# Splitting an inverse transform and a projection into groups of 16 passes among other matrix products

## The chip, the core and the metric

The kernel runs on one core of one Trainium2 chip. The metric is the device time of one execution in microseconds (us); three runs of the kernel before gave 5190.26 us in the median (5189.91 to 5219.42). The engines carry the profile's names: PE is TensorE (matrix products; PEld its weight loads), DVE is VectorE, ACT is ScalarE, POOL is GpSimd, SP the engine that here only issues loads and stores. Each engine runs its instructions in the order in which the program writes them.

## What is computed

Two layers on an image batch of 4 x 64 x 256 x 256 in fp32. The first, which the change touches, is a normalised convolution block with products in the frequency domain of 8 x 8 patches:

```python
def layer0(x):                                   # x: (4, 64, 256, 256)
    y = group_norm(x)
    hidden = einsum('bchw,oc->bohw', y, w1)      # 1x1, 64 -> 384 channels
    hidden = depthwise_3x3(hidden, w_dw)
    q, k, v = split(hidden, 3, axis=1)           # 128 channels each
    out = irfft2(rfft2(patches(q)) * rfft2(patches(k)))
    out = layer_norm_over_channels(unpatch(out)) * ln_w + ln_b
    return x + einsum('bchw,oc->bohw', v * out, w_out)   # projection and residual
```

The second layer is a GRU that runs column by column over the result; nothing of it changes.

## The kernel before

**Blocks.** Layer 0 runs over 32 blocks of 32 image rows (the GRU follows it). A block holds 128 patches, 64 in each half of the partitions; xq is its normalised input with a border of one pixel, 100 numbers for each 8 x 8 patch.

**Stages of a block, in the order of TensorE's program.** The loop `for n in range(NBLK + 1)` does, for block n:

1. *First chunk of 1x1 units.* Sixteen calls of `pointwise` (`unit_of`): 16 passes each (a product in fp32 is two passes in the trace, so 8 products), then one copy of 1024 numbers per partition from the ring into h. ACT makes most copies, DVE units 3 and 9. DVE meanwhile runs steps of block n-1's layer norm, one for each `go()`.
2. *`circular(n, 0, ..)`.* Four rounds of `products`: two `transform`s of 64 passes with matrices t from memory (depthwise filter and Fourier transform in one), a copy by ACT, two multiplications by DVE. `inverse` turns a pair of these products into z: 48 passes of 512 columns into four banks, then one ACT copy of 2048 numbers. The first of a block's four inverses runs in this stage.
3. *Second chunk of units*, with half 0 of block n-1's projection after unit 11 (`project`, then `add_residual` on DVE, then `leave`), and the second inverse after unit 15.
4. *`circular(n, 1, ..)`* with the third inverse in it. The fourth waits in the list `pending`.
5. *Third chunk of units*, for v. `flush()` after unit 3 runs the fourth inverse. DVE copies units 4, 6 and 15. The steps of `go()` at units 6 and 7 are statistics of z, 16 instructions each, and they need the z of the fourth inverse.
6. *Half 1 of block n-1's projection*, 64 passes of 512 columns from v of block n-1, then `go(1)`, `add_residual(1, ..)`, `go(3)`. The first of these steps closes the statistics (moments) and makes the first of eight passes over z (subtract the mean, multiply by the reciprocal deviation, in quarters).
7. *v's products.* Eight calls of `values` of 64 passes each with matrices t; `keep_values` copies them by ACT, k = 0 and 1, 3 and 4, 6 and 7 in one copy of 2048 numbers, k = 2 and 5 alone. Among them ACT and DVE normalise the next block's input (`normalize`), and `leave` makes statistics of the finished half and stores it.

**The ring.** All results of stages 1 to 7 go through one PSUM tile `psring` of eight banks, given out in turn by `psum(banks)`: two banks for a unit, a transform or a v product alone, four for an inverse, a projection or two v products. A request for four starts at bank 0 or 4. A bank is written again when its last reader is done, so with pairs in turn TensorE can be four units ahead of their copies.

**h, z, v** are single buffers. A v product k reads 16 of h's 128 channels for all units, and part b of a projection reads a quarter of v (32 features), which the products 2b and 2b + 1 of the new block overwrite.

**Order.** `InOrder` keeps every engine's instructions in program order, and as all of them are recorded by its one helper, every row of the profile has its line, L157. The rows are told apart by their tiles: `psring<-w_sb,xq` is a unit, `psring<-h,t` with 32 columns of weights a transform and with 64 a v product, `psring<-wk,g_sb` the inverse, `psring<-v,wo_sb` the projection. `wk<-psring,wk` of 512 columns is `add_residual`, and of 1024 the products.

Of the kernel before, what the change touches and what calls it, by code (L numbers as in the profile page):

```python
# [18 lines left out]
P = 128  # L19
# [6 lines left out]
NBLK = B * W // 32  # L26
# [136 lines left out]
def tile_conv_then_gru(  # L163
# [47 lines left out]
    with tc.tile_pool(name="xa", bufs=5) as xa, tc.tile_pool(name="sta", bufs=1) as sta, tc.tile_pool(  # L211
# [18 lines left out]
        for i in range(32):  # L230
# [3 lines left out]
            for k in range(4):  # L234
                at = slice(32 * k, 32 * k + 9)
# [40 lines left out]
    with layer0 as s:  # L276
# [1 line left out]
        tp = s.enter_context(tc.tile_pool(name="tp", bufs=4))  # L278
        ps2 = s.enter_context(tc.tile_pool(name="ps2", bufs=1, space=PSUM))
        ring = ps2.tile([P, 8, 512], F32, tag="ring", name="psring")  # L280
        place = [0]

        def psum(banks=2):

            at = place[0] + (-place[0]) % banks
            place[0] = (at + banks) % 8
            return ring[:, at % 8 : at % 8 + banks]

# [41 lines left out]
        def matrix(n, kind, k):  # L330

            fetch(n * 24 + order.index((kind, k)) + 4)
            return matrices.pop((n, (kind, k)))

        def unit_of(n, chunk, unit, vector):

# [21 lines left out]
        def pointwise(n, chunk, unit, vector):  # L358

            unit_of(n, chunk, unit, vector)()  # L360
# [53 lines left out]

        def flush():
            while pending:
                pending.pop(0)()

        def inverse(n, pair):

            pz = psum(4)
            for i in range(2):
                slot = PAIRS[pair % 2][i]
                both = wk[:, slot : slot + 2].rearrange("p t (r s g n) -> p r g t s n", r=2, g=2, n=NJ)
                for part in range(2 - i):
                    for g in range(2):
                        for c in range(4):
                            at = slice(32 * c, 32 * c + 32)
                            nc.tensor.matmul(
                                pz[g * 64 : g * 64 + 64, c].rearrange("p (t s n) -> p t s n", t=2, n=NJ),  # L430
                                lhsT=g_sb[at, part, i, :],
                                rhs=both[at, part, g],
                                start=i == part == 0,
                                stop=i == 1,
                                tile_position=(32 * c, g * 64),
                            )
            nc.scalar.copy(
                z[:, :, 32 * pair : 32 * pair + 32], pz.rearrange("p c (f n) -> p n (c f)", n=NJ)
            )

        def values(n, k, pv):

# [12 lines left out]
        def keep_values(k, count, pv):  # L455
            nc.scalar.copy(
                v[:, :, 16 * k : 16 * (k + count)], pv.rearrange("p x (f n) -> p n (x f)", n=NJ)
            )
# [78 lines left out]
            return xr  # L537

        def project(n, u):
            po = psum(4)  # L540
            y = v.rearrange("p n (b k) -> p b n k", k=32)
            for b in range(4):
                for r in range(4):
                    for s in range(2):
                        n0 = 32 * u + 16 * s
                        nc.tensor.matmul(
                            po[s * 64 : s * 64 + 64, r].rearrange("p (n k) -> p n k", k=32),
                            lhsT=wo_sb[32 * r : 32 * r + 32, b, :],
                            rhs=y[32 * r : 32 * r + 32, b, n0 : n0 + 16],
                            start=b == 0,  # L550
                            stop=b == 3,
                            tile_position=(32 * r, s * 64),
                        )
            return po

        def add_residual(u, po, xr):
            for g in range(2):
                grid = xr[g].rearrange("p (h r) (n c) -> p h n r c", h=2, c=8)
                for half in range(2):
                    nc.vector.tensor_tensor(  # L560
                        grid[:, half],
                        po[:, 2 * g + half].rearrange("p (n r c) -> p n r c", r=4, c=8),
                        grid[:, half],
                        ALU.add,
                    )
# [34 lines left out]
        def go(steps=1):  # L600
            for _ in range(steps):
                if norm:
                    next(norm, None)

        for n in range(NBLK + 1):
            last = n == NBLK
            more = not last and n // 8 + 1 < B
            if last:
                for _ in norm:
                    pass  # L610
                for i in range(4):
                    gated(n - 1, i)
                for u in range(2):
                    xr = residual(n - 1, u)
                    add_residual(u, project(n - 1, u), xr)
                    leave(n - 1, u, xr)
                break
            if more:
                look(n, 0)
            for unit in range(16):  # L620
                if unit < 14:
                    pointwise(n, 0, unit, unit in (3, 9) if norm else unit % 2)
                elif unit == 14:
                    last_two = [unit_of(n, 0, unit, False)]
                else:
                    last_two.append(unit_of(n, 0, unit, False))
                    for span in ((0, 16), (16, P)):
                        for copy in last_two:
                            copy(*span)
                if unit in (0, 3, 6, 9, 12):  # L630
                    go()

            def beside_first(sp):
                if n and sp < 3:
                    gated(n - 1, sp)
                go()
                if n and sp == 3:
                    gated(n - 1, sp)
                if more and sp == 1:
                    count(n, 0)  # L640

            go()
            circular(n, 0, beside_first)
            crossed(1)
            go(8)
            xr = [None, None]
            if n:
                xr[0] = residual(n - 1, 0)
            for unit in range(16):
                pointwise(n, 1, unit, unit in (7, 12))  # L650
                if n and unit == 11:
                    add_residual(0, project(n - 1, 0), xr[0])
                if n and unit == 13:
                    leave(n - 1, 0, xr[0])
                if more and unit == 9:
                    count(n, 4)
            flush()
            norm = layer_norm(n)

            def beside(sp):  # L660
                go()
                if more and sp == 2:
                    count(n, 8)

            circular(n, 1, beside)
            image = None
            if n:
                xr[1] = residual(n - 1, 1)
            for unit in range(16):
                pointwise(n, 2, unit, unit in (4, 6, 15))  # L670
                if more and unit == 2:
                    count(n, 12)
                    if n % 8 == 7:
                        t = wk[:, 3]
                        nc.gpsimd.dma_start(t[:, 0 : 2 * P].rearrange("p (a q) -> p a q", a=2), sums)
                        image = norm_of_pieces(nc, st0, t, lambda: psum()[:, :, 0], eps, sc0[:, n // 8 + 1])
                if image and unit in (4, 8, 12):
                    next(image)
                if unit == 3:
                    flush()  # L680
                if unit in (6, 7):
                    go()
                if unit % 4 == 3 and n + 1 < NBLK:
                    load(n + 1, unit // 4)
            po = project(n - 1, 1) if n else None
            go(1)
            if n:
                add_residual(1, po, xr[1])
            go(3)
            for k in range(8):  # L690
                if k in (0, 3, 6):
                    pv = psum(4)
                    values(n, k, pv[:, 0:2])
                elif k in (1, 4, 7):
                    values(n, k, pv[:, 2:4])
                    keep_values(k - 1, 2, pv)
                else:
                    pv = psum()
                    values(n, k, pv)
                    keep_values(k, 1, pv)  # L700
                if k in (1, 2, 4) and n + 1 < NBLK:
                    normalize(n + 1, k // 2)
                if k == 5 and n:
                    leave(n - 1, 1, xr[1])
                if k == 5 and n + 1 < NBLK:
                    normalize(n + 1, 3)
                if k in (6, 7):
                    go()
            fetch(n * 24 + 28)
# [251 lines left out]
```

## Time and profile before

| | us |
|---|---|
| median of 3 runs | 5190.26 |
| the profiled execution | 5200.96 |
| its span, first to last instruction | 5199.2 |
| TensorE clock granted, mean | 0.99 of full |

The profile is one execution. A busy share is a share of that span; a TensorE row shows when passes start and how long each takes to pass through, and passes on different tiles of the array overlap, so its end is modelled. In the timeline, consecutive instructions of one kind are one row: start, length from the first start to the last end, how many, and in brackets the idle time before the row and what ended it. The sums of TensorE by kind, over all blocks:

| passes | count | mean of one, ns |
|---|---|---|
| 1x1 units | 24576 | 273 |
| transforms | 32768 | 274 |
| v's products | 16384 | 223 |
| inverse | 6144 | 600 |
| projection | 4096 | 607 |

And the copies and additions beside them:

| | count | mean, ns |
|---|---|---|
| ACT h, whole unit (1024) | 1243 | 1029 |
| ACT h, 896 and 128 of a unit | 64 and 64 | 916 and 276 |
| DVE h, whole unit | 229 | 1214 |
| ACT z of an inverse (2048) | 128 | 1866 |
| ACT v, two products (2048) | 96 | 1867 |
| ACT v, one product (1024) | 64 | 1002 |
| DVE add_residual, each of four | 256 | 682 |
| DVE pass over a quarter of z | 256 | 2279 |

### The profile page before, as it was taken

To read this page: it belongs to the slowest core of one execution; us is meant where nothing else is said; L and a number is where in the kernel's file an instruction comes from. 1 tells how busy PE (TensorE), PEld (TensorE's weight loads), DVE (VectorE), ACT (ScalarE), POOL (GpSimd) and SP (SyncE) were. 2 spreads that over 40 slices of the span, in tenths; PEclk is the share of its full clock that TensorE was granted. 3 is DMA by queue.
4 is the path that set the end of the run, shared out by engine and by line. 5 is a ranking of instruction groups with operands and counts; after the bars stand their busy time and mean duration, and the time that the engine had idled before them with its cause. 6 is when DMAs were issued, how large, how long until landed. Compare 5 with 4: busy or idle time off the path is not lost.

```text
span 5199.2 us, 275863 instructions
## 1 busy us (share of the span) xinstructions
PE 4911.1 (94%) x127092; PEld 4202.2 (81%) x127092; DVE 4038.0 (78%) x7000; ACT 3348.7 (64%) x4253; POOL 1724.5 (33%) x1723
## 2 busy tenths in 40 slices
PE   4999999999999999999999999999789999999999
PEld 3887888788888888888887888888578888888888
DVE  4678888877888887788887777878667777777777
ACT  3666667666666766666666666667466666666665
POOL 0233333333333333333333323223333333333333
PEclk9999999999999999999999999999899999999999
DMA  7566665666666666666656656655443333333332
GB/s 266 148 171 178 185 180 166 168 175 169 171 188 173 171 170 175 172 178 180 186 160 162 151 155 164 168 159 151 111 123 99 100 98 99 100 100 100 97 100 71
DMA packets 421174, 784.55 MB, mean 151 GB/s; under 512 B 32604, under 2 KB 295552, under 8 KB 417632
## 3 DMA queue, kind: packets, MB, share of 16 engines
q1 hardware_dynamic: 366464, 533.76, 38.1%
q0 software_dynamic: 53264, 232.55, 15.3%
q8 instruction: 997, 16.33, 1.4%
q14 instruction: 161, 1.32, 0.1%
q10 hardware_dynamic: 288, 0.58, 0.0%
HBM read 622.72 MB, written 144.05 MB: 147 GB/s over the span
## 4 chain that ended last, share of the span: by engine, by line
PE 78%; DVE 7%; issue 5%; ACT 5%; DMA 4%; POOL 1%; ACTq 0%; POOLq 0%; SPq 0%; DVEq 0%
PE psring L157 57%; PE pshz L157 7%; PE pshr L157 6%; PE psni L157 5%; PE pshn L157 3%; DMA t<-t_all 2%; ACT z L157 2%; DVE n L157 2%; ACT v L157 1%; DVE wk L157 1%; ACT xq L157 1%; DVE st L157 1%; DVE g L157 1%; DVE z L157 1%; DMA wk<-in_sums 1%
## 5 line engine op out<-in xcount | busy, mean ns | idle before, releaser
L157 PEld LDWEIGHTS psring<-h,t 100*32 100x32 f32 x49152 | 1383.5, 119 | 249.1 <-issue 195.7
L157 PE MATMUL psring<-h,t 100*32 100x128 f32 x49152 | 1464.3, 257 | 96.7 <-issue 59.0
L157 PEld LDWEIGHTS psring<-w_sb,xq 64*100 64x100 f32 x24576 | 1372.6, 164 | 123.1 <-issue 89.7
L157 PE MATMUL psring<-w_sb,xq 64*100 64x128 f32 x24576 | 1430.4, 273 | 34.2 <-issue 21.6
L157 ACT COPY h<-psring 100x1024 f32<-100x1024 f32 (+2 forms) x1371 | 1234.1, 988 | 336.8 <-PE psring L157 335.9
L157 DVE TENSOR_TENSOR wk<-psring,wk 128x1024 f32<-128x1024 f32 (+1 forms) x768 | 759.5, 1037 | 461.5 <-PE psring L157 320.2
L157 POOL TENSOR_TENSOR v<-v,z 128x2048 f32<-128x2048 f32 x128 | 582.7, 4557 | 658.6 <-DVE wk L157 603.0
L157 DVE TENSOR_TENSOR z<-z,moments 128x2048 f32<-128x2048 f32 x256 | 578.0, 2279 | 2.3
L157 POOL TENSOR_TENSOR wk<-wk 128x1024 f32<-128x1024 f32 x128 | 303.4, 2371 | 618.7 <-DVE wk L157 596.6
L157 POOL TENSOR_TENSOR raw<-raw,st 128x512 f32<-128x512 f32 x256 | 303.1, 1184 | 530.6 <-DVE st L157 471.5
L157 ACT COPY z<-psring 128x2048 f32<-128x2048 f32 x128 | 238.9, 1866 | 348.8 <-PE psring L157 248.2
L157 PE MATMUL pshr<-st,wi 64*64 64x144 f32 (+7 forms) x12240 | 429.7, 269 | 6.7 <-DVE st L157 6.7
L157 DVE COPY h<-psring 100x1024 f32<-100x1024 f32 x229 | 277.5, 1214 | 198.7 <-PE psring L157 192.7
L157 PE MATMUL psni<-st,wi 64*64 64x144 f32 (+7 forms) x12240 | 428.6, 269 | 1.3 <-issue 1.3
L157 PE MATMUL pshz<-st,wi 64*64 64x144 f32 (+7 forms) x12240 | 428.8, 269 | 0.1
L157 ACT ACTIVATE z<-pshz,b_rz 128x288 f32<-128x288 f32 (+7 forms) x510 | 242.0, 475 | 281.3 <-PE pshz L157 275.8
L157 ACT COPY wk<-psring 128x1024 f32<-128x1024 f32 x256 | 259.5, 1014 | 249.5 <-PE psring L157 214.4
L157 DVE BATCH_NORM_STATS2 lnst<-z 128x6 f32<-128x128 f32 x2048 | 416.8, 282 | 0.0
L157 ACT COPY v<-psring 128x2048 f32<-128x2048 f32 (+1 forms) x160 | 243.3, 1521 | 251.0 <-PE psring L157 251.0
L157 PEld LDWEIGHTS pshr<-st,wi 64*64 64x64 f32 x12240 | 370.0, 133 | 41.1 <-DVE st L157 9.8
L157 PEld LDWEIGHTS psni<-st,wi 64*64 64x64 f32 x12240 | 369.7, 133 | 31.3 <-issue 0.7
L157 PE MATMUL psring<-wk,g_sb 32*64 32x512 f32 x6144 | 382.1, 600 | 9.2 <-issue 5.9
(96 smaller groups left out, 6170.2 us busy)
## 6 DMA issues: line engine op xcount, KB each, us to landing
t<-t_all SPq DMA_DIRECT2D x768, 400.0 KB
xq<-in_xh POOLq DMA_DIRECT2D x128, 800.0 KB, 6.1
wk<-in_x SPq DMA_DIRECT2D x256, 256.0 KB
x<-wk POOLq DMA_DIRECT2D x256, 256.0 KB, 5.4
seen<-in_x POOLq DMA_DIRECT2D x96, 512.0 KB, 7.6
raw<-x SPq DMA_DIRECT2D x128, 256.0 KB
raw<-x SPq DMA_DIRECT2D x256, 128.0 KB
out<-raw SPq DMA_DIRECT2D x128, 256.0 KB
```

The source lines that it names most:

```text
L157: return self.tc.keep_in_program_order(got(*args, **kwargs))
```

## The change

Three things are rearranged; no arithmetic is added or left out.

- `inverse` and `project` become generators that stop after every 8 products (16 passes). The fourth inverse of a block is issued in three groups, after units 3, 4 and 5 of the third chunk, and its copy to z follows the third. Half 1 of the projection is issued in four: one after unit 15, and one each after v's products k = 0, 2 and 4. `add_residual` follows the fourth; `go(4)` stands in one piece before v's products, and `leave` moves from k = 5 to k = 6. Elsewhere the generators run through at once.
- While an inverse or a projection is open, its four banks are held and `psum()` gives the other four in turn, two pairs; `release()` sets the turn on.
- v's products take two banks each and are copied one by one; the next block's normalisations stand at k = 0, 2, 4. The copies of units 14 (ACT) and 15 (DVE) of the third chunk are each made in two parts, channels 0 to 15 of both first, as the first chunk's are already.

```diff
-        place = [0]
+        place, held, turn = [0], [None], [0]
 
-        def psum(banks=2):
+        def psum(banks=2, hold=False):
 
+            if held[0] is not None:
+                at = (held[0] + 4) % 8 + 2 * turn[0]
+                turn[0] ^= 1
+                return ring[:, at : at + banks]
             at = place[0] + (-place[0]) % banks
+            if hold:
+                held[0], turn[0] = at % 8, place[0] % 4 // 2
             place[0] = (at + banks) % 8
             return ring[:, at % 8 : at % 8 + banks]
...
+        def release():
+            place[0] = (held[0] + 4) % 8 + 2 * turn[0]
+            held[0] = None
...
         def flush():
             while pending:
-                pending.pop(0)()
+                for _ in pending.pop(0)():
+                    pass
 
         def inverse(n, pair):
 
-            pz = psum(4)
+            pz = psum(4, True)
...
+                    yield
             nc.scalar.copy(
                 z[:, :, 32 * pair : 32 * pair + 32], pz.rearrange("p c (f n) -> p n (c f)", n=NJ)
             )
+            release()
...
         def project(n, u):
-            po = psum(4)
+            po = psum(4, True)
...
-            return po
+                yield po
...
                 if n and unit == 11:
-                    add_residual(0, project(n - 1, 0), xr[0])
+                    for po in project(n - 1, 0):
+                        pass
+                    add_residual(0, po, xr[0])
+                    release()
...
             for unit in range(16):
-                pointwise(n, 2, unit, unit in (4, 6, 15))
+                if unit < 14:
+                    pointwise(n, 2, unit, unit in (4, 6))
+                else:
+                    last_two = (last_two if unit == 15 else []) + [unit_of(n, 2, unit, unit == 15)]
+                if unit == 15:
+                    for span in ((0, 16), (16, P)):
+                        for copy in last_two:
+                            copy(*span)
...
                 if unit == 3:
-                    flush()
+                    spread = pending.pop(0)()
+                if unit in (3, 4, 5):
+                    next(spread)
+                if unit == 5:
+                    for _ in spread:
+                        pass
...
-            po = project(n - 1, 1) if n else None
-            go(1)
+            parts = project(n - 1, 1) if n else None
             if n:
-                add_residual(1, po, xr[1])
-            go(3)
+                next(parts)
+            go(4)
             for k in range(8):
-                if k in (0, 3, 6):
-                    pv = psum(4)
-                    values(n, k, pv[:, 0:2])
-                elif k in (1, 4, 7):
-                    values(n, k, pv[:, 2:4])
-                    keep_values(k - 1, 2, pv)
-                else:
-                    pv = psum()
-                    values(n, k, pv)
-                    keep_values(k, 1, pv)
-                if k in (1, 2, 4) and n + 1 < NBLK:
+                pv = psum()
+                values(n, k, pv)
+                keep_values(k, 1, pv)
+                if k in (0, 2, 4) and n:
+                    po = next(parts)
+                if k in (0, 2, 4) and n + 1 < NBLK:
                     normalize(n + 1, k // 2)
-                if k == 5 and n:
+                if k == 4 and n:
+                    add_residual(1, po, xr[1])
+                    release()
+                if k == 6 and n:
                     leave(n - 1, 1, xr[1])
                 if k == 5 and n + 1 < NBLK:
                     normalize(n + 1, 3)
```

More of the change, by code (lines that the diff above doesn't have):

```diff
@@ L614, in tile_conv_then_gru @@
                     xr = residual(n - 1, u)
-                    add_residual(u, project(n - 1, u), xr)
+                    for po in project(n - 1, u):
+                        pass
+                    add_residual(u, po, xr)
+                    release()
                     leave(n - 1, u, xr)
@@ L679, in tile_conv_then_gru @@
                 if unit == 3:
-                    flush()
+                    spread = pending.pop(0)()
[3 more added lines that the diff above has]
+                    for _ in spread:
+                        pass
                 if unit in (6, 7):
@@ L684, in tile_conv_then_gru @@
                     load(n + 1, unit // 4)
-            po = project(n - 1, 1) if n else None
-            go(1)
+            parts = project(n - 1, 1) if n else None
             if n:
-                add_residual(1, po, xr[1])
-            go(3)
+                next(parts)
+            go(4)
             for k in range(8):
-                if k in (0, 3, 6):
-                    pv = psum(4)
-                    values(n, k, pv[:, 0:2])
-                elif k in (1, 4, 7):
-                    values(n, k, pv[:, 2:4])
-                    keep_values(k - 1, 2, pv)
-                else:
-                    pv = psum()
-                    values(n, k, pv)
-                    keep_values(k, 1, pv)
-                if k in (1, 2, 4) and n + 1 < NBLK:
+                pv = psum()
[4 more added lines that the diff above has]
+                if k in (0, 2, 4) and n + 1 < NBLK:
                     normalize(n + 1, k // 2)
-                if k == 5 and n:
+                if k == 4 and n:
+                    add_residual(1, po, xr[1])
+                    release()
+                if k == 6 and n:
                     leave(n - 1, 1, xr[1])
```

## The prediction

> **What bounds the kernel now.** I read the page's engine line and chain of waits first, then the groups kept apart by shape, then the timeline of one block (1992 to 2046 us), last the start times of single passes in it.
>
> ```profile
> PE 4911.1 (94%) x127092; PEld 4202.2 (81%) x127092; DVE 4038.0 (78%) x7000; ACT 3348.7 (64%) x4253; POOL 1724.5 (33%) x1723
> PE 78%; DVE 7%; issue 5%; ACT 5%; DMA 4%; POOL 1%; ACTq 0%; POOLq 0%; SPq 0%; DVEq 0%
> ```
>
> TensorE sets the end over most of the span; VectorE is the next share of the chain. Averages do not show where, so here are the two groups of weight loads that the change touches, with their idle time:
>
> ```profile
> L157 PEld LDWEIGHTS psring<-w_sb,xq 64*100 64x100 f32 x24576 | 1372.6, 164 | 123.1 <-issue 89.7 <-ACT z L157 10.9 <-DVE h L157 7.4
> L157 PEld LDWEIGHTS psring<-h,t 100*64 100x64 f32 x16384 | 491.9, 138 | 71.8 <-issue 54.7 <-ACT v L157 12.7 <-DMA t<-t_all 2.0
> ```
>
> Waits for a copy out of the ring are small: 10.9 (the inverse's z), 7.4 (units copied by VectorE), 12.7 us (v's copies), 31.0 in all. "issue" has no releaser and stays. Now the stretch itself, TensorE, ScalarE and VectorE:
>
> ```profile
> 1994.16 2.83 PE L157 MATMUL psring<-wk,g_sb 32*64 32x512 f32 x48
> 1996.92 1.99 PE L157 MATMUL psring<-w_sb,xq 64*100 64x128 f32 x32
> 1997.15 1.86 ACT L157 COPY z<-psring 128x2048 f32<-128x2048 f32 x1 [1.74 <-PE psring L157]
> 1999.07 2.10 PE L157 MATMUL psring<-w_sb,xq 64*100 64x128 f32 x32 [0.15 <-ACT z L157]
> ...
> 2002.37 6.37 DVE L157 BATCH_NORM_STATS2 lnst<-z 128x6 f32<-128x128 f32 x32
> ...
> 2008.95 3.69 PE L157 MATMUL psring<-v,wo_sb 32*64 32x512 f32 x64
> 2009.13 1.22 DVE L157 COPY h<-psring 100x1024 f32<-100x1024 f32 x1 [0.39 <-ACT h L157]
> ...
> 2011.95 2.23 DVE L157 TENSOR_TENSOR z<-z,moments 128x2048 f32<-128x2048 f32 x1
> 2012.57 15.79 PE L157 MATMUL psring<-h,t 100*64 100x64 f32 x512
> 2014.10 2.47 DVE L157 TENSOR_TENSOR wk<-psring,wk 128x512 f32<-128x512 f32 x4
> 2016.49 6.81 DVE L157 TENSOR_TENSOR z<-z,moments 128x2048 f32<-128x2048 f32 x3
> ...
> 2023.21 2.47 DVE L157 BATCH_NORM_STATS2 bn<-wk 128x6 f32<-128x512 f32 x4
> ...
> 2025.71 0.37 DVE L157 BATCH_NORM_AGGREGATE st<-bn 128x2 f32<-128x48 f32 x1
> 2026.00 1.04 DVE L157 TENSOR_SCALAR xq<-xq,sc 128x1600 f32<-128x1600 f32 x1
> ...
> 2026.96 6.81 DVE L157 TENSOR_TENSOR z<-z,moments 128x2048 f32<-128x2048 f32 x3
> 2028.29 15.06 PE L157 MATMUL psring<-w_sb,xq 64*100 64x128 f32 x256
> ...
> 2033.69 1.22 DVE L157 COPY h<-psring 100x1024 f32<-100x1024 f32 x1
> ```
>
> To see: from unit 15's copy (2009.13) to the copy of unit 3 of the next block (2033.69) VectorE has no gap. Unit 7 of that block needs unit 3's ring pair. Call t the start of the last 1x1 pass (2008.75): unit 3's copy ends at t+26.16. Over the blocks measured so (29) that end has the median t+26.16 and unit 7 starts at t+26.93: VectorE is under 0.8 us from binding.
>
> **The change part by part** (us per block; 32 blocks, 31 with a projection in them).
>
> *More changes between tile shapes.* Passes are the same in number. The inverse becomes I16 U16 I16 U16 I16: two more pairs of changes 1x1-inverse. The projection becomes four groups with v's products between: three more pairs. Start to start the inverse takes 2.76 (1994.16 to 1996.92), the projection 3.62 (2008.95 to 2012.57): 16 passes more cost 0.86, so the inverse has 2.76 - 3 x 0.86 = 0.18 that is no passes. By single starts a 1x1 stretch has as much: after a 1x1 pass the next shape comes 0.200 later and not 0.103 (+0.10), its second round of eight +0.05, after the last inverse pass the 1x1 comes 0.518 later and not 0.38 (+0.14), its second pair +0.08: 0.37 a pair of changes. Projection to v: +0.14 and +0.05; v to another shape is only seen going to 1x1, 0.152 for 0.052 (+0.10), and +0.05 in the first round: 0.34. Cost 2 x 0.37 x 32 = 23.5 and 3 x 0.34 x 31 = 31.6, sum 55. The Trainium skill (TensorEngine Tiling (Array Packing), Key Properties) says that a change of tiling mode drains TensorE; that speaks against the change but gives no price. A sum that left it out would be -31 (the waits alone); with the rows it is +24. I take the rows. Bounds of v-to-projection, unseen in this order: 0 to 0.15 more, that is 0 to +14 us.
>
> *Waits removed.* z's 10.9 and VectorE's 7.4: units 4 and 5 now lie inside the inverse, but its copy starts two units later and the held half leaves units two pairs: unit 8 asks for z's banks. By starts, z's copy (1.86) ends some 0.2 after unit 8 could start, so I count half: -9. v's 12.7 goes wholly: eight single copies (1.00 each) for three of 1.87 and two of 1.00, 8.0 for 7.6 on ScalarE, +0.4 that its idle before (5.12 at 2016.57) covers.
>
> *Units 14 and 15 in halves.* ScalarE pays 276 + 916 ns for the 1029 of a whole copy, +0.16; VectorE has no such row, between 0 and +0.3, I take 0.15. Both lie beside part one of the projection and v's first product; without that cover they would delay the first v product, which starts at t+1.25 where the first halves should be done at t+0.7 and the unit-14 banks free at t+1.1.
>
> *Moved queues.* Normalisations at k = 0, 2, 4 instead of 1, 2, 4: xq's load was issued 17 us earlier (1995.51) and lands in 6.1; nothing. leave's four x stores on POOL pass one memset of 0.12, its statistics pass xq's scaling on VectorE; SP's order of loads is unchanged. Nothing.
>
> *The add waits longer, and VectorE queues behind it.* Before, add_residual reads the projection at t+5.34, long after it is done. Now its fourth part follows v's k = 4. From single starts: first v product t+1.25; a v product 1.90, a part with its changes 1.20; k = 1, 3 and 5 start at 4.34, 9.34, 14.29; the fourth part's last pass ends at t+14.4. VectorE by then has done unit 15's copy (1.35), the moments (1.7) and four scalings (2.24 each), so it stands from t+12.3: idle 2.1. Behind the add (2.39 to its successor) are xq's scaling 0.96, the statistics 2.79, three scalings 6.73, then unit 3's copy 1.22: it ends at 14.4 + 14.1 = t+28.5 against 26.16. TensorE could start unit 7 at t+26.3 and waits to 28.55. Unit 9's copy ends 5.49 later (two VectorE operations and itself), t+34.0, and unit 13 waits for it, starting at 34.05 against a median of 32.17 and a mean of 32.60 before. Stalls without releaser in k = 0 to 4 add 0.16 in the mean. So +1.6 in the mean (+1.9 by the median) x 31 = 50 to 58. This already contains the projection's changes and v's waits, which lie under it. Later VectorE has 0.5 in hand at the next transform, still 0.2.
> A rule weighs here: TensorE: Matmul & The Clock Gate (Architectural detail) says that VectorE's queue is strictly first in, first out. If scalings could pass the waiting add, only the TensorE sum (+24) would stand; with the rule the add holds them. The trace's VectorE order is the program's at every step, so I take the rule.
>
> *Sum.* VectorE's chain +54, the inverse's changes +23.5, its waits and VectorE's -9, rest of the ScalarE pacing in those 12 units about -6 (they take 12.16 in the mean, 11.02 at best, the like 12 of the second chunk 10.66): +62. The profiled execution took 5200.96 (span 5199.2), 0.2% over the median of 5190.26; the sum is a difference, so it stands on the median: 5252.
>
> **Rivals.**
> - *TensorE alone counts* (VectorE finds time, for instance because the fourth part ends earlier). +55 for changes, -31 waits: 5214. For: chain 78% TensorE. Against: no VectorE gap in the stretch.
> - *Not slower: the inserted groups fill waits.* Place: units 6 to 15 of the third chunk and v's products, where TensorE waits on copies. The 12 units exceed 10.66 by 1.5 in the mean, v's products their least by 0.87 (16.59 to 15.72): 2.4 x 32 = 76. If all of that is the ring's, -76 + 55 = -21: 5169. It decides when over 1.75 a block vanish and the add isn't late. Against: most of that excess is "issue" or loads.
> - *Worse:* the held half also stalls v or units (a unit waits when its pair's copy is late, about 0.5 a block): 5275.
> - That the change does not do what it says, I exclude: order on each engine is the program's.
>
> **How the numbers follow.** VectorE's chain 0.62 (5235 to 5270), TensorE alone 0.17, filled waits 0.11, worse 0.10. About 1%, 52 us, is what a measurement can tell from no change, so 5242 and 5138 are the limits. VectorE's case lies to about three quarters above 5242, with the worse one 0.56 slower; faster by over 1% needs more than every wait: 0.04; the rest 0.40 within. The range leaves out the filled waits and the far end of the worse case: 5195 to 5285; the likeliest case alone is 5235 to 5270.
>
> **What would show it.** Right: add_residual's VectorE row now has idle time before it, released by TensorE, some 2 us a block (60 in all); "DVE h" in the 1x1 weight-load row grows from 7.4 to over 60; "ACT v" in v's row goes to nearly 0; between groups of 16 passes the start-to-start time is 1.05. Wrong: VectorE still without a gap there, or unit 7 starting below t+27.5; then the sum falls to TensorE's. If a group of 16 costs under 0.9 start to start, the drain term is too large.

## The result, and the profile after

The changed kernel takes 5289.55 us in the median of six runs (5278.2 to 5306.63), the kernel before 5199.66 (six runs, 5189.91 to 5219.42): 1.0172 times as long, 95% interval 1.0149 to 1.0196. It is 90 us slower where 62 were forecast, and lies 4.5 us beyond the range. The 5252 of the forecast stood on the 5190.26 of three runs of the kernel before; of the 37.5 us between 5252 and 5289.55, 9.4 are that starting point and 28 the forecast itself. The profiled execution (span 5304.9) is the slowest of the six, so its difference to the profiled execution before is larger, 105.7.

The page's engine line and its chain of waits, after:

```profile
PE 4958.9 (93%) x127092; PEld 4196.9 (79%) x127092; DVE 4045.1 (76%) x7032; ACT 3384.3 (64%) x4381; POOL 1722.1 (32%) x1723
PE 71%; DVE 15%; issue 5%; DMA 5%; ACT 2%; POOL 1%; ACTq 0%; SPq 0%; POOLq 0%; DVEq 0%
PE psring L157 51%; PE pshz L157 7%; PE pshr L157 6%; PE psni L157 5%; DVE z L157 3%; PE pshn L157 3%; DMA t<-t_all 3%; DVE wk L157 3%; DVE bn L157 2%; DMA seen<-in_x 2%; DVE n L157 2%; ACT z L157 2%; DVE st L157 1%; DVE g L157 1%; DVE h L157 1%
```

The passes are as many as before, and VectorE is hardly busier. But its share of the chain went from 7% to 15%, and two names are new among its lines: `DVE bn` (statistics of rows) and `DMA seen` (the load of the next image's rows). The groups by shape say who waited (busy us, mean ns, then idle us before the group and what ended it). First three rows after, then the row of add_residual before:

```profile
L157 PEld LDWEIGHTS psring<-w_sb,xq 64*100 64x100 f32 x24576 | 1384.8, 166 | 240.0 <-DVE h L157 102.9 <-issue 94.7 <-ACT h L157 26.0
L157 PEld LDWEIGHTS psring<-h,t 100*64 100x64 f32 x16384 | 492.1, 138 | 116.4 <-issue 84.6 <-ACT h L157 25.2 <-ACT v L157 5.4
L157 DVE TENSOR_TENSOR wk<-psring,wk 128x512 f32<-128x512 f32 x256 | 159.1, 683 | 243.2 <-PE psring L157 126.5 <-issue 108.9 <-DMA wk<-in_x 7.8
```

```profile
L157 DVE TENSOR_TENSOR wk<-psring,wk 128x512 f32<-128x512 f32 x256 | 158.8, 682 | 176.1 <-issue 114.5 <-PE psring L157 53.8 <-DMA wk<-in_x 7.8
```

In the units' row the wait for VectorE's copies grew from 7.4 to 102.9; in v's row the wait for ScalarE's copies of v fell from 12.7 to 5.4. The 25.2 for `ACT h` there is new, but it is idle time of weight loads beside the projection's first group: v's first product starts at t+1.24 in every block, as forecast (1.25). Before add_residual VectorE now waits 126.5 for TensorE (53.8 before). The timeline of one block shows how they hang together (rows of TensorE and VectorE; t, the start of the block's last 1x1 pass as in the forecast, is 3344.13):

```profile
3344.33 1.11 PE L157 MATMUL psring<-v,wo_sb 32*64 32x512 f32 x16
3345.37 2.09 PE L157 MATMUL psring<-h,t 100*64 100x64 f32 x64
...
3347.41 9.08 DVE L157 TENSOR_TENSOR z<-z,moments 128x2048 f32<-128x2048 f32 x4
...
3357.24 1.11 PE L157 MATMUL psring<-v,wo_sb 32*64 32x512 f32 x16
...
3358.36 2.48 DVE L157 TENSOR_TENSOR wk<-psring,wk 128x512 f32<-128x512 f32 x4 [1.87 <-PE psring L157]
...
3364.03 6.36 PE L157 MATMUL psring<-w_sb,xq 64*100 64x128 f32 x112
...
3364.57 6.75 DVE L157 TENSOR_TENSOR z<-z,moments 128x2048 f32<-128x2048 f32 x3
...
3371.24 1.22 DVE L157 COPY h<-psring 100x1024 f32<-100x1024 f32 x1
...
3372.51 5.49 PE L157 MATMUL psring<-w_sb,xq 64*100 64x128 f32 x96 [2.12 <-DVE h L157]
```

VectorE has done its four passes at 3356.5 and stands until the projection's fourth group (3357.24) is through, 1.87 us. Everything behind the add is late by that, unit 3's copy too, and TensorE stands 2.12 us before unit 7 (x112 is seven units).

From the starts of single passes, means over 30 blocks, in us a block:

| from | to | before | after |
|---|---|---|---|
| t, last 1x1 pass of a block | unit 7 of the next | 27.22 | 28.77 |
| unit 7 | unit 13 | 5.35 | 5.99 |
| third chunk, unit 0 | t | 18.50 | 19.31 |
| all the rest of a block | | 62.26 | 62.64 |
| a block | | 113.33 | 116.71 |

3.38 us x 31 is 105, the whole difference of the two spans: by rows 48, 20, 25 and 12. The forecast had the first row right (50 to 58 for the first two together); the second and third came out larger than forecast. The last is within what single executions differ by: in the profiles of the thirteen kernels it lies between 61.5 and 62.8.

### The profile page after: what moved, and what is told of

Its sections match the earlier page's. It is cut to its first block, busy times and chain, and to the rows that moved or that the text cites. A ratio compares the mean times of both kernels' runs of the same rounds, so it can differ in the third digit from the quotient of the medians.

```text
span 5304.9 us, 276055 instructions
## 1 busy us (share of the span) xinstructions
PE 4958.9 (93%) x127092; PEld 4196.9 (79%) x127092; DVE 4045.1 (76%) x7032; ACT 3384.3 (64%) x4381; POOL 1722.1 (32%) x1723
## 4 chain that ended last, share of the span: by engine, by line
PE 71%; DVE 15%; issue 5%; DMA 5%; ACT 2%; POOL 1%; ACTq 0%; SPq 0%; POOLq 0%; DVEq 0%
PE psring L157 51%; PE pshz L157 7%; PE pshr L157 6%; PE psni L157 5%; DVE z L157 3%; PE pshn L157 3%; DMA t<-t_all 3%; DVE wk L157 3%; DVE bn L157 2%; DMA seen<-in_x 2%; DVE n L157 2%; ACT z L157 2%; DVE st L157 1%; DVE g L157 1%; DVE h L157 1%
## 5 line engine op out<-in xcount | busy, mean ns | idle before, releaser
L157 PEld LDWEIGHTS psring<-w_sb,xq 64*100 64x100 f32 x24576 | 1384.8, 166 | 240.0 <-DVE h L157 102.9
L157 ACT COPY h<-psring 100x1024 f32<-100x1024 f32 x1403 | 1241.5, 970 | 497.6 <-PE psring L157 494.1
L157 PE MATMUL psring<-w_sb,xq 64*100 64x128 f32 x24576 | 1450.5, 274 | 103.8 <-DVE h L157 76.1
L157 DVE COPY h<-psring 100x1024 f32<-100x1024 f32 (+2 forms) x261 | 279.8, 1082 | 212.5 <-PE psring L157 212.2
L157 PE MATMUL psring<-wk,g_sb 32*64 32x512 f32 x6144 | 402.8, 615 | 13.3 <-issue 9.2
L157 ACT COPY v<-psring 128x1024 f32<-128x1024 f32 x256 | 259.3, 1013 | 191.0 <-PE psring L157 190.8
```

Source lines behind the costliest of these rows:

```text
L157: return self.tc.keep_in_program_order(got(*args, **kwargs))
```

## The experiments

Eleven kernels ran, each beside the kernel before on the same chip; intervals are at 95%. The chips differ from one experiment to another, so a ratio tells more than a difference of two times.

### One half of the change at a time

*inverse_only* is the kernel before with the spread fourth inverse and its held banks:

```diff
                 if unit == 3:
-                    flush()
+                    spread = pending.pop(0)()
+                if unit in (3, 4, 5):
+                    next(spread)
+                if unit == 5:
+                    for _ in spread:
+                        pass
```

> The fourth inverse in three groups among units 4 and 5, its banks held; projection and v's products as before. Two theories of what this half costs. Changes of tile shape alone, less the waits on z that go: about +9 us on the kernel before (5209). A second cost, that the held half leaves the units two pairs, so that unit 6 has to wait for unit 4's copy, which VectorE makes only after statistics that wait for a load (seen): the changed kernel took 0.82 us a block more here, so +26 us (5226), and the stretch from unit 4 to unit 6 takes 4.2 us in blocks without such statistics (24 to 31) and up to 7 in the others.

Measured 5234.81 us, 1.0069 (1.0040 to 1.0097) of the kernel before: +36 us, not +9. The second theory holds. Unit 4 to unit 6 took up to 7.4 us, 5.03 in the mean, in line with the changed kernel (5.01), and 4.19 in the eight blocks without such statistics.

*projection_only* is the changed kernel with `flush()` after unit 3 in place of the spread inverse.

> The projection in four groups among v's products, v copied one by one; the inverse whole. If VectorE's late add is the main cost, unit 7 of the first chunk still starts at t+28.4 and the time lies 60 to 70 us over the kernel before (5260 to 5270). If the inverse's part made most of the loss, it lies within 35 us of it.

Measured 5267.97, 1.0119 (1.0096 to 1.0143): +62; unit 7 starts at t+28.83 in the mean, at t+28.38 at the earliest. The halves sum to 98 and the whole change made 90, which agrees within the intervals: they are two separate costs.

### Is it VectorE's wait, or the splitting?

*projection_whole* keeps the held banks, the single copies and the add after k = 4, and takes only the breaks out of the projection:

```diff
             if n:
-                next(parts)
+                for po in parts:
+                    pass
             go(4)
...
-                if k in (0, 2, 4) and n:
-                    po = next(parts)
```

> As projection_only, but the four groups follow one another after unit 15, so that add_residual, still after k = 4 and with the banks held until then, finds its sums ready. VectorE's wait for the last group is the cause: then VectorE has no gap, unit 3's copy ends near t+26.4, unit 7 starts below t+27, and the time is that of the kernel before or up to 15 us below it (5185 to 5200). The held half, or the single copies, or the add's later place in itself are the cause: then it stays at 5240 or above.

Measured 5205.88, 1.0011 (0.9997 to 1.0025). The 62 us are gone; the few us of gain that were allowed for did not come. The timeline (TensorE and VectorE, t = 3124.94):

```profile
3125.14 3.69 PE L157 MATMUL psring<-v,wo_sb 32*64 32x512 f32 x64
...
3128.20 9.08 DVE L157 TENSOR_TENSOR z<-z,moments 128x2048 f32<-128x2048 f32 x4
3128.76 15.27 PE L157 MATMUL psring<-h,t 100*64 100x64 f32 x512
...
3137.20 2.48 DVE L157 TENSOR_TENSOR wk<-psring,wk 128x512 f32<-128x512 f32 x4
...
3150.08 1.22 DVE L157 COPY h<-psring 100x1024 f32<-100x1024 f32 x1
...
3151.36 1.89 PE L157 MATMUL psring<-w_sb,xq 64*100 64x128 f32 x30 [1.03 <-DVE h L157]
```

The add follows the four passes with no gap, at t+12.26 and not t+14.23. v's products run through in 15.27 us, and still unit 7 waits 1.03 us: VectorE's work from t to unit 3's copy fills 26.4 us whatever TensorE does, and takes what the single copies might have brought (tested below).

*five_steps_first* leaves the projection split and gives VectorE work in the wait:

```diff
-            go(4)
+            go(5)
...
-                if k in (6, 7):
+                if k == 7:
                     go()
```

> The changed kernel whole, with one of VectorE's passes over z moved ahead of the add (go(5), and one step fewer after k = 6), so that VectorE works where it waited. VectorE's wait is the cause: unit 3's copy ends near t+26.3, unit 7 waits 0.1 to 0.3 us, and the time falls by 70 to 85 us to 5205 to 5220. Changes of tile shape are the cause: it falls by less than 20 us.

Measured 5227.39, 1.0045 (1.0028 to 1.0063): 62 us below the changed kernel (66 by the ratios), less than the 70 to 85 foreseen but far from the other theory's 20. Unit 7 comes at t+26.81 in the mean. What is left over the kernel before (+23) is no more than the inverse's half.

*three_steps_first* makes the suspected wait longer by one pass: `go(3)`, and `k in (5, 6, 7)`.

> The changed kernel whole, with one of VectorE's passes over z moved behind the add (go(3), and a step more after k = 5): the suspected wait is made 2.24 us longer. If VectorE's chain is all of it, unit 7 starts at t+30.6 and the time rises by 2.24 x 31 = 69 us to 5360. If TensorE's clock is gated after the wait, as in the 12 of 30 blocks of the changed kernel where units 7 to 13 took 6.99 and not 5.5 us, then a wait of 4.4 us brings it in nearly every block: 1.46 us x 18 more, so 5385, with half clock in the rows after unit 7.

Measured 5387.02 (two runs), 1.0356 (1.0326 to 1.0386). Unit 7 starts at t+30.58 to 30.59 in most blocks. Of the 97 us over the changed kernel the longer wait itself makes 2.24 x 31 = 69. For the other 28 see TensorE's clock. Each row below is a stretch of time: its bounds and length, busy time and number of instructions of PE, PEld, DVE, ACT and POOL, the granted clock as a share of full speed, the DMA share and GB/s. First the changed kernel, the wait and what follows it in one block, then in another; then three_steps_first.

```profile
3598.00:3602.70 4.70, 2.69 (x50) 2.47 (x46) 4.70 (x4) 3.24 (x4) 0.00 (x0) 1.00 0.50 187
3602.80:3606.20 3.40, 3.40 (x42) 3.40 (x44) 3.40 (x2) 1.65 (x2) 0.00 (x0) 0.67 0.02 5
...
3367.60:3372.40 4.80, 2.79 (x52) 2.58 (x48) 4.80 (x4) 3.35 (x4) 0.00 (x0) 1.00 0.47 168
3372.50:3375.90 3.40, 3.39 (x62) 3.39 (x64) 3.40 (x2) 1.94 (x2) 0.00 (x0) 1.00 0.00 0
```

```profile
3200.00:3205.20 5.20, 1.85 (x32) 1.64 (x28) 5.20 (x4) 2.90 (x3) 0.00 (x0) 0.96 0.20 75
3205.30:3208.70 3.40, 3.40 (x36) 3.40 (x38) 3.40 (x2) 1.01 (x1) 0.00 (x0) 0.57 0.00 0
3208.70:3212.10 3.40, 3.40 (x66) 3.40 (x64) 3.35 (x3) 2.58 (x3) 0.00 (x0) 1.00 0.01 2
```

After the wait, 42 passes in 3.40 us at a granted clock of 0.67, where another block has 62 at 1.00. In the changed kernel that befell 11 of the 30 blocks that follow a split projection (the expectation says 12), each with units 7 to 13 in 6.9 to 7.0 us; the records of the clock show a stretch of 3.41 us at 0.5 right there in each of the 11 and in none of the others. With the longer wait 27 of 30 blocks took 6.7 us or more, and the mean clock over the span fell from 0.986 to 0.979 (0.990 in the kernel before). Five_steps_first, without the wait, has no such stretch between units 7 and 13 and takes 5.43 us there in the mean, the changed kernel 5.99: 0.55 x 31 = 17 us of its time is the clock.

### What makes units 4 to 6 slow

The changed kernel around units 4 to 6 (TensorE, VectorE):

```profile
1451.22 1.66 DVE L157 BATCH_NORM_STATS2 lnst<-z 128x6 f32<-128x128 f32 x8
...
1453.46 1.12 PE L157 MATMUL psring<-w_sb,xq 64*100 64x128 f32 x16
1454.51 1.11 PE L157 MATMUL psring<-wk,g_sb 32*64 32x512 f32 x16
1455.44 1.29 DVE L157 BATCH_NORM_STATS2 bn<-seen 128x6 f32<-128x512 f32 x2 [2.55 <-DMA seen<-in_x]
...
1457.05 1.16 DVE L157 COPY h<-psring 100x1024 f32<-100x1024 f32 x1
1458.26 8.98 PE L157 MATMUL psring<-w_sb,xq 64*100 64x128 f32 x160 [0.55 <-DVE h L157]
```

Unit 4 is through TensorE at about 1454.5. VectorE copies it at 1457.05, because the statistics that stand before it in the program waited 2.55 us for the rows of the next image. With four pairs unit 8 would ask for that bank; with two it is unit 6. *inverse_count_later* moves those statistics behind the copy:

```diff
-                if more and unit == 2:
+                if more and unit == 4:
                     count(n, 12)
```

> As inverse_only (5235), with the last statistics of the next image's rows, which wait for their load, behind VectorE's copy of unit 4 and not ahead of it. The held half makes that wait matter: units 4 to 6 take 4.2 us in every block, and the time falls by 0.8 x 24 = 20 us to 5215; what is left over the kernel before are the changes of tile shape. If not: it stays within 6 us of 5235.

Measured 5215.20, 1.0037 (1.0024 to 1.0049): as foreseen; unit 4 to unit 6 falls to 4.30 us in the mean (least 4.19). By the medians the wait on `seen` is about half of the inverse's cost, and +19 us (13 to 26) stay. This is less sure than it looks: the interval overlaps that of inverse_only (1.0040 to 1.0097), and in the two profiles the third chunk as a whole takes the same time, 19.26 and 19.25 us in the mean. Twenty blocks with statistics are 0.6 us shorter (19.16 and 18.57), but the three that end an image (n = 7, 15, 23) are 3.8 us longer; there the edit also puts off the closing of that image's statistics. So it is shown that the held half turns the late copy into TensorE's wait at unit 6; what that costs in all is about 20 us by the medians and 12 in those twenty blocks.

### A version faster than both

If VectorE's chain takes what the single copies bring, that chain has to lose a copy to show it. *whole_unit3_scalar* is projection_whole with unit 3 of the first chunk copied by ScalarE:

```diff
-                    pointwise(n, 0, unit, unit in (3, 9) if norm else unit % 2)
+                    pointwise(n, 0, unit, unit == 9 if norm else unit % 2)
```

> As projection_whole (5206; single v copies, projection and inverse in one piece), with unit 3 of the first chunk copied by ScalarE, so that VectorE's chain no longer ends before unit 7. If VectorE's chain is what hid the gain of the single copies: unit 7 starts near t+25.4, unit 13 waits for unit 9's copy until t+31, and the next transform starts about 1 us earlier, 5165 to 5175. If ScalarE becomes the bound in the first chunk: 5200 or more.

Measured 5178.08, 0.9964 (0.9950 to 0.9977): 19 us faster than the kernel before by the ratio, though not quite the 5165 to 5175 expected. At best unit 7 starts at t+25.21; but its median is t+26.77, since v's products were slower than in their best blocks. (The profiled execution, 5201.5, is the slowest of thirteen.)

*whole_unit3_count* adds the edit of inverse_count_later.

> As whole_unit3_scalar, with the statistics behind unit 4's copy as in inverse_count_later. With four pairs in the ring that wait cost only some 3 us in all before, so within 8 us of whole_unit3_scalar.

5188.24, 0.9977 (0.9969 to 0.9985): no further gain, which fits that the full ring had hidden that wait. It is 10 us over whole_unit3_scalar, 7 by the ratios, with intervals that overlap.

*before_unit3_scalar* is the same edit on the kernel before.

> The kernel before with the one edit that ScalarE copies unit 3 of the first chunk. If the gain of whole_unit3_scalar needs the single copies of v too: the copies of two products still hold up v's k = 3 and 6 and unit 2, so 5 us below the kernel before at most (5195 to 5200). If the edit alone makes it: 5175 to 5185.

5179.72, 0.9995 (0.9982 to 1.0008), beside a median of 5182.59 for the kernel before on that chip: by the ratio no difference, so the edit alone does not make it.

*split_unit3_scalar* asks for the price of the splitting where VectorE no longer covers it: five_steps_first with the inverse whole and unit 3 on ScalarE.

> As whole_unit3_scalar, but with the projection in four groups among v's products and five of VectorE's passes ahead of the add, as in five_steps_first; the inverse whole. Where VectorE no longer ends before unit 7, the three more pairs of changes of tile shape must show: the next block's units start at t+19.9 and not t+19.0, 0.88 us x 31 = 27 us, so about 5205. If the changes cost nothing once VectorE is out of the way: within 8 us of whole_unit3_scalar (5178).

5162.41, on the chip of before_unit3_scalar, 0.9960 (0.9940 to 0.9979) beside 0.9964 for whole_unit3_scalar: the expected 27 us do not show, though the least time from t to the next unit is 19.90 with groups and 19.02 without, as worked out. The means are 20.51 and 20.62: without groups v's products lose elsewhere. From the first to the last pass of k = 5, 6 and 7 it takes 2.17, 2.15 and 2.21 us in the mean in whole_unit3_scalar and 1.89, 1.88 and 1.91 in split_unit3_scalar, at best 1.81 in both. (The profile of the second is its fastest execution, that of the first its slowest; but projection_whole, whose profile is the fastest of twenty, has 2.03, 2.04 and 2.20 there, so it is not the choice of execution.)

*whole_half_the_loads* leaves out half of the matrices of v's products, 400 KB each, and uses the others twice, so its result is another one:

```diff
-        order += [(2, k) for k in range(8)]
+        order += [(2, k) for k in (0, 2, 4, 6)]
...
+            if kind == 2 and k % 2:
+                return matrices.pop((n, (2, k - 1)))
```

> As whole_unit3_scalar, but a block loads only four of the eight matrices of v's products; k = 1, 3, 5 and 7 take those of k - 1 (part of the computation is changed: half of v comes from other filters). The question is why the projection in groups cost nothing in split_unit3_scalar: from t to the next block's first unit the two take the same 20.5 us in the mean, though the least is 19.9 with groups and 19.0 without. If matrices that arrive late hold up v's products when these follow one another without a break, and the groups give them time, then with half the loads the mean from t to the next unit falls from 20.6 to 19.6 or below, and the time to 5145 or below. If the stalls without a releaser have nothing to do with these loads: the mean stays at 20.3 to 20.6.

5145.00 (four runs), 0.9896 (0.9854 to 0.9939); t to the next unit falls to 19.29 in the mean (least 19.02), and k = 5 to 7 take 1.83, 1.92 and 1.86. So the stalls without a releaser in v's products hang on these loads, and groups of the projection between the products avoid them too: what the groups cost in changes of shape they saved there. That the change speeds up other loads as well is not excluded.

But it is not the matrices that come late, as the expectation put it. The 64 passes of a product read one matrix, which comes in one transfer, and the stalls fall in the middle of a product, here after 8 passes of k = 7 (TensorE, whole_unit3_scalar; below it, a row of the page's DMA queues):

```profile
1219.30 8.38 PE L157 MATMUL psring<-h,t 100*64 100x64 f32 x276
1230.15 1.85 PE L157 MATMUL psring<-h,t 100*64 100x64 f32 x56 [2.46 <-issue]
...
q8 instruction: 997, 16.33, 1.4%
```

Queue q8 brings instructions, 997 packets of 16,384 bytes, one for every 256 of the 255,323 instructions on record for TensorE. One of these packets moves from 1227.50 to 1228.58, and the passes go on at 1230.15. In blocks 1 to 30 of this profile products 5 to 7 have 21 steps of over 0.2 us from one pass to the next, 23.7 us together; all 21 end 1.2 to 1.8 us after such a packet has landed, where only 12% of all these passes lie so. In split_unit3_scalar they are 7 (4.8 us), with half the loads 6 (4.1 us), and each of them lies so too. TensorE thus waits there for its own instructions. A product takes 128 of them in some 1.8 us, so eight in a row use up a packet in about 3.6 us (an estimate from these numbers), and a group of the projection in between or fewer loads of data make a late packet rarer. How the data's loads delay a packet is not shown.

## Why the forecast was wrong

- *The add waits longer, and VectorE queues behind it.* Right, and shown by two edits that only lengthen or fill that wait (three_steps_first, five_steps_first) and one that takes it away with the groups (projection_whole). In the median the fourth group's last pass starts at t+13.64 and ends at about t+14.2 (worked out: 14.4); unit 7 starts at t+28.39 (28.55). In the mean 1.55 us a block, 48 us, of the 50 to 58. Where the clock stayed full, unit 7 to unit 13 took 5.49 us in the mean, as worked out (5.50).
- *The rule that VectorE's queue is first in, first out* (the Trainium skill, TensorE: Matmul & The Clock Gate, Architectural detail) was rightly taken over the TensorE sum of +24: no pass over z went ahead of the waiting add, 1.87 us of idle time in the row.
- *More changes between tile shapes.* The size was right pass by pass: a group of 16 starts the next shape 1.044 later (1.05 forecast), and from a v product to the projection, unseen before, a pass starts 0.152 later, as to a 1x1 unit. For the inverse the least time of the third chunk went from 17.29 to 18.02, 0.73 for the two pairs of changes put at 2 x 0.37. For the projection the price is real in the best blocks, 0.88 (19.90 for 19.02) against 1.02 worked out, but in the mean v's products made it good. That the stalls called "issue" would stay as they were was wrong: in v's products they are waits for instructions, and groups make them rarer.
- *Waits removed*, the step that failed. It credited the spread inverse with 9 us of waits on z and VectorE's copies, and the sum another 6, so that this half stood at +8.5. In the profile the third chunk took 25 us more (0.81 x 31), and the half alone cost +36 (21 to 51): the changes of shape in full, and no waits gone on balance. z's wait only moved, to unit 8: units 6 to 8 take 2.15 in the median, 1.83 before. And VectorE's copies, with two pairs in the ring, became a new wait on statistics that wait for a load. Of blocks 1 to 31, the eight without such statistics take 0.44 us more than before in the third chunk, the twenty that have them and do not end an image 1.30: the difference, 0.86 x 20 = 17 us, is an estimate of that wait. The forecast had it only as the general case of its worse rival.
- *The clock*, a term that was not in the sum, the second thing that failed: +17 us. The Trainium skill (TensorE: Matmul & The Clock Gate, Why this matters for your kernels) warns of idle gaps over about 3 us; here one of 2.1 us was enough in 11 of 30 blocks.
- The other marks came as written: add_residual's idle time for TensorE +73 us (about 60 forecast), "DVE h" over 60 (102.9), "ACT v" down to 5.4. The rival of filled waits was right that something was filled, but it was waits for instructions, and it shows in the time only where the add is not late (split_unit3_scalar).

So where the forecast had +54 for the chain and +8.5 for the inverse, the two profiles have 48 (chain), 20 up to unit 13 (17 of it the clock), 25 (the inverse: 23 for shapes, 2 for waits on balance) and 12 in the rest of a block, no more than single executions differ by: 105. The medians of six runs give 90, so how the 28 us beyond the forecast split between clock and inverse is known only roughly.

## What to carry to other kernels

A reader of a matmul's result that is moved closer to its last group waits in an in-order engine, and everything queued behind it moves too: look at that engine's next deadline, and place work of its own before the add (one step more was worth some 62 us here). Holding half of a ring halves the time that every other copy may be late, so look for copies that are queued behind a load. Splitting a run of passes costs a fixed time for each change of tile shape (0.3 to 0.4 us there and back here), but that can be made good where a long run of short passes waits for its instructions.

## What was not expected of the hardware

- A wait of TensorE of 2.1 us was followed by 3.41 us at half its clock in 11 of 30 blocks, one of 4.4 us (three_steps_first) in 27 of 30; a block loses some 1.5 us by it on top of the wait.
- TensorE can stand in the middle of a run of passes, with no releaser in the profile, until 1.2 to 1.8 us after a packet of its instructions has landed. These stalls of up to 2.9 us make k = 5 to 7 of v's products take some 2.2 us in the mean for 1.81 at best when eight follow one another (whole_unit3_scalar), and 1.83 to 1.92 when a group of the projection (some 1.1 us) stands after k = 0, 2 and 4, or when half the matrices are not loaded.
